# Moving a pair of two-column vector instructions from the stage that prepares a projection into the projection itself

## The chip, the cores and the metric

The kernel runs on one core of a Trainium2 chip. The metric is the device time of one execution in microseconds (us); the median of several executions is compared.

## What is computed

The input x has 1024 rows of 512 numbers. It is normalized row by row (layer norm), and two branches work on the result xn:

```python
xn = _layernorm(x, axis=-1)
s = _L0_attn_ref(xn, ...)        # attention
g = _silu(_L0_ffn_ref(xn, ...))  # feed-forward with 4-bit weights
x = x + s * g
```

The attention has 32 query heads and 8 heads of keys and values, each 128 wide, with four query heads to one key head:

```python
q = (x @ Wq.T)...; k = (x @ Wk.T)...; v = (x @ Wv.T)...
q = _rmsnorm(q, q_norm_w)
k = _rmsnorm(k, k_norm_w)
scores = jnp.einsum('bkgqd,bksd->bkgqs', qg, k) / math.sqrt(HD)
bias = jnp.where(rel > 0, NEG_INF, slopes[:, :, None, None] * rel)
attn = jax.nn.softmax(scores + bias[None], axis=-1)
out = jnp.einsum('bkgqs,bksd->bkgqd', attn, v)
return out.reshape(b, s, H * HD) @ Wo.T
```

Queries and keys are normalized by head, the values are not.

## The kernel before

Four stages follow one another: the layer norm with the gate and up projections of the feed-forward branch; its down projection; the query, key and value projections (about 220 to 505 us of the span); and the attention with the output projection and the gating. This case is about the third, and about the seams before and after it.

**Projections.** A list `projections` holds twelve of them, numbered k = 0 to 11: for each of four pairs of key heads one of keys and values (`kv`; k = 0, 3, 6, 9) and two of queries (`q`). A projection works through eight tiles of 128 rows, t = 0 to 7. `tile(t)` multiplies the tile of xn by the weights into one accumulator `ps`: twelve matmuls, since both operands are split into a high and a low half and three of the four products are taken. The accumulators have two tags ("o" for odd tiles, "m" for even ones) with two buffers each. ACT (ScalarE) then copies the queries or keys into `f` (L515) and sums their squares (L517). Of a `kv` projection, ACT also casts the values to 16 bits (`v16`, L521), and DVE (VectorE) takes the rest that the cast left out (L522). `v16` has three buffers; one step later both halves are stored to memory by two DMAs (L527). `f` has three buffers of four tiles.

**Factors of the values.** So that the values fit 16 bits, the columns of the value weights are scaled before the projection by a factor `al` for each column, found from their squares, and the attention's result is scaled back by the reciprocal. This goes in steps, and `prepare(k + 1, t)` gives the next projection's steps to the tiles of the current one: squares at t = 0, sums (`norms`) at t = 1, `scale` at t = 3, which also stores `al` to memory by a DMA (`ald`, L483), `factors` at t = 5, which loads it back by a DMA with heads as columns (`ri`, L490), and `undo` at t = 7. `undo` takes the reciprocal of `ri`, 128 x 2 numbers (L495), and multiplies it by a constant into two columns of `rv` (L496). `rv` is read by the attention alone (`heads_hi`, L807, and `heads_lo`, L813). The weights of the next projection are split into halves meanwhile (`split`, L502 on ACT and L503 on DVE). For projection 0 the same steps are given to the last iterations of the down projection (`undo` in its last one).

**Deferred steps.** What follows a tile's sums is put off by a table of due times: `finish_step()` ends each tile and runs what is due. Every four tiles `queue_half` enters the inverse root (L535, L84, L85 on DVE, Newton steps on POOL, that is GpSimd), the normalization on POOL (L556), and the split of the normalized rows into 16-bit halves `q` or `k` on DVE (`halves`, L568 and L569; `a16`, five buffers). One step later SP issues a transposing DMA (L574, into `tr`, five buffers) and two steps after that the store (L579 for queries, L582 for keys). So the halves of a projection's tiles fall four to eight tiles after them, that is into the next projection.

**Order.** Every engine runs its instructions in the order in which the program gives them; the order is written out by hand. All DMAs leave from one queue, SP's. At the start of k = 9 SP also issues the loads of the first keys, values and queries of the attention (L709, L713, L717), 512 KB each. From k = 10 on, the first steps of the attention run between the tiles.

Of the kernel before, what the change touches and what calls it, by code (L numbers as in the profile page):

```python
# [31 lines left out]
HT = NT // 2  # L32
# [35 lines left out]
def attention_gated_by_ffn_kernel(ctx, tc, x, gu_w, gu_z, gu_s, dn_w, dn_z, dn_s, wq, wkv, wo, qnw, knw, out):  # L68
# [374 lines left out]
    def finish_step():  # L443

        for f in finishing.pop(clock[0], ()):
            f()
        clock[0] += 1
# [141 lines left out]
    def prepare(k, t):  # L589

        if k < len(projections):
            p = projections[k]
            if t == 0:
                p.squares()
            elif t == 1:
                p.norms()
            elif t == 3:
                p.scale()
            elif t == 5:
                p.factors()  # L600
            elif t == 7:
                p.undo()
            if p.kind == "q" and 2 <= t < 6:
                p.split(t - 2)
            elif p.kind == "kv" and 4 <= t < 6:
                p.split(2 * t - 8)
                p.split(2 * t - 7)
# [7 lines left out]
    for it in range(3, NI):  # L615
        if it < 3 + 2 * KT:
            projections[(it - 3) // KT].load((it - 3) % KT)
        last = it == NI - 1
        gu_unit(
            it,  # L620
            None,
            it + 1 if not last else None,
            meanwhile={NI - 2: lambda: dn_dequant(0, ve), NI - 1: down_begin}.get(it, lambda: None),
            total=not last,
        )
        if it in (NI - 5, NI - 4):
            prepare(0, it - NI + 5)
        if it == NI - 3:
            dn_load(0)
            dn_load(1)  # L630
        if last:
            dn_load(2)
            dn_split_h(0, 1)
# [3 lines left out]
    for it in range(NI):  # L637
        for tb in range(2):
# [17 lines left out]
            if tb:  # L656
                if it in (1, 2):
                    gu_total((NI - 1, None), it - 1)
                elif it == 3:
                    gu_finish(0)  # L660
                elif it == 4:
                    gu_finish(1)
                elif it == 5:
                    norm_weights()
                elif it == NI - 5:
                    prepare(0, 3)
                elif it >= NI - 4:
                    prepare(0, 8 - NI + it)
# [15 lines left out]
    def queue_half(p, half):  # L684

        last = p is projections[-1]

        def due(steps, i, f):
            t = half * HT + i
            c = TILES - early + BS * (NB * (1 + t // 2) + FINISH_BLOCK) + 4 * (t % 2) if last else clock[0] + i  # L690
            finishing.setdefault(c + steps, []).append(f)

        due(0, 0, lambda: p.inverse(half))
        for i in range(3):
            due((i + 1) // 2, 0, lambda i=i: p.newton(half, i == 2))
        for i in range(HT):
            t = half * HT + i
            due(4, i, lambda t=t: p.halves(t))
            due(2, i, lambda t=t: p.normalize(t))
# [7 lines left out]
    def load_keys(g):  # L707
        kT[g] = ap1.tile([P, NT, 2, P], F16, tag="kT", name=f"kT{g}")
        sp.dma_start(kT[g].rearrange("p t a k -> p t (a k)"), kd[g].rearrange("t p c -> p t c"))  # L709

    def load_values(g):
        vT[g] = ap1.tile([P, NT, 2, HD], F16, tag="vT", name=f"vT{g}")
        sp.dma_start(vT[g].rearrange("p t a d -> p t (a d)"), vd[g])  # L713

    def load_queries(g, qb):
        qT[g, qb] = ap1.tile([P, NQT, 2, NH, P], F16, tag="qT", name=f"qT{g}_{qb}")
        sp.dma_start(  # L717
            qT[g, qb].rearrange("p t a g q -> p t (a g q)"), qd[g][qb * NQT : (qb + 1) * NQT].rearrange("t p c -> p t c")
        )
# [12 lines left out]
    def relative(g):  # L732

        trel[g] = ap1.tile([P, S], F32, tag="trel", name=f"trel{g}")
        ge.tensor_scalar(trel[g], nrel, rc, float(SLOPES[g * NH + NH - 1]), ALU.mult, ALU.mult)
# [190 lines left out]
    for k, p in enumerate(projections):  # L926
        if k == len(projections) - 3:
            load_keys(0)
            load_values(0)
            load_queries(*blocks[0])  # L930
            relative(0)
        for t in range(NT):
            prepare(k + 1, t)
            if k + 2 < len(projections) and t < KT:
                projections[k + 2].load(t)
            p.tile(t)
            finish_step()
            if t % HT == HT - 1:
                queue_half(p, t // HT)
            if k >= len(projections) - 2 and t % 2 == 0:  # L940
                step(early)
                early += 1
# [46 lines left out]
```

## Time and profile before

| what | us |
|---|---|
| median of 3 runs | 1102.81 |
| lowest and highest of them | 1100.63, 1103.02 |
| the profiled execution | 1098.13 |
| its span in the profile | 1096.4 |
| PE (TensorE, matmuls) busy | 1043.1 |
| DVE busy | 878.5 |
| ACT busy | 761.5 |
| POOL busy | 393.3 |
| the four RECIPROCALs (L495) begin between | 212.4 and 424.5 |

The span runs from the first to the last instruction of the program; what the execution takes beyond it lies around it. In the lines of a timeline the first two numbers are the start, counted from the span's start, and the duration of one row; then come the engine ("SPq" is SP's queue, which only issues), the line of the program, the operation, what it writes and reads, shapes and the number of instructions in the row. In brackets stands the idle time of the engine before it and what ended that. In the table of waits, a line says who waited for whom, and the total, the number and the longest of these waits. The chain of waits follows the work that ended last back from its end, at each step to what released it.

### The profile page before, as it was taken

How to read it: one execution, taken by the hardware profiler on the slowest of the kernel's cores; microseconds unless marked ns; L12 is line 12 of the kernel's file. 1: busy time of each engine (PE TensorE's matmuls, PEld its weight loads, DVE VectorE, ACT ScalarE, POOL GpSimd, SP SyncE). 2: the span in 40 equal slices, each digit the busy share in tenths (PEclk: the TensorE clock that was granted, in tenths of full speed). 3: DMA queues.
4: the chain of work that ended last, by engine and by line, in shares of the span. 5: the costliest groups of instructions: out<-in, count | busy, mean ns of one | idle time of the engine just before them, and what ended most of it. 6: DMA issues, size and time to landing. Idle time of an engine off the chain costs nothing.

```text
span 1096.4 us, 18629 instructions
## 1 busy us (share of the span) xinstructions
PE 1043.1 (95%) x5900; PEld 763.1 (70%) x5900; DVE 878.5 (80%) x1703; ACT 761.5 (69%) x2031; POOL 393.3 (36%) x545
## 2 busy tenths in 40 slices
PE   7999999999999999898899899999999999999997
PEld 6677678878888887675566667666666676676664
DVE  7888897537687786787789798898898987969984
ACT  5767543446666474677779688796796887868962
POOL 2566553126778787560202304004021030032222
PEclk9999999999999999899999999999999999999999
DMA  6122345146998979979989999899999998999993
GB/s 196 57 87 91 93 128 166 53 132 144 218 229 183 230 179 250 245 163 227 215 170 203 187 223 212 195 206 192 195 210 188 200 221 175 195 220 208 239 193 114
DMA packets 461632, 198.11 MB, mean 181 GB/s; under 512 B 395810, under 2 KB 421726, under 8 KB 461534
## 3 DMA queue, kind: packets, MB, share of 16 engines
q1 hardware_dynamic: 461534, 196.93, 81.6%
q8 instruction: 46, 0.75, 0.3%
q14 instruction: 52, 0.43, 0.1%
HBM read 71.03 MB, written 29.36 MB: 92 GB/s over the span
## 4 chain that ended last, share of the span: by engine, by line
PE 61%; DMA 13%; DVE 10%; ACT 8%; issue 5%; POOL 3%; SPq 0%; DVEq 0%; ACTq 0%; POOLq 0%
DMA pT<-p 12%; PE gu_ps L249 6%; PE ps_q L105 4%; PE ps_q L106 4%; PE ps_q L107 4%; PE s L105 4%; PE s L106 3%; PE s L107 3%; PE av L105 3%; PE op L105 3%; PE op L106 3%; PE op L107 3%; PE av L106 3%; PE av L107 3%; ACT p L770 3%
## 5 line engine op out<-in xcount | busy, mean ns | idle before, releaser
L779 DVE SCALAR_TENSOR_TENSOR p<-pf,row,p 128x1024 f16<-128x1024 f32 (+7 forms) x256 | 219.9, 859 | 69.3 <-ACT p L770 67.0
L770 ACT ACTIVATE p<-pf,row 128x1024 f16<-128x1024 f32 (+7 forms) x256 | 197.0, 770 | 66.6 <-DMA pT<-p 63.2
L760 ACT ACTIVATE pf<-pf,row 128x1024 f32<-128x1024 f32 (+7 forms) x256 | 197.2, 770 | 42.1 <-DVE row L759 40.2
L730 POOL TENSOR_TENSOR wol<-wor,woh 128x512 fp32r<-128x512 f32 x32 | 58.1, 1816 | 427.4 <-ACT woh L729 379.0
L759 DVE CUSTOM_DVE_ANT_0 pf<-s,trel,cs 128x1024 f32<-128x1024 f32 (+7 forms) x256 | 207.3, 810 | 3.0 <-PE s L107 2.3
L105 PE MATMUL av<-pT,vT 128*128 128x256 f16 (+1 forms) x640 | 170.8, 267 | 20.5 <-DMA pT<-p 19.9
L106 PE MATMUL av<-pT,vT 128*128 128x256 f16 (+1 forms) x640 | 168.2, 263 | 0.0
L107 PE MATMUL av<-pT,vT 128*128 128x256 f16 (+1 forms) x640 | 168.1, 263 | 0.0
L105 PEld LDWEIGHTS <-vT 128*128 128x128 f16 x640 | 62.4, 97 | 101.7 <-issue 80.6
L105 PE MATMUL s<-kT,qT 128*128 128x512 f16 (+3 forms) x384 | 125.3, 326 | 6.9 <-DVE row L759 6.6
L106 PE MATMUL s<-kT,qT 128*128 128x512 f16 (+3 forms) x384 | 125.2, 326 | 0.0
L107 PE MATMUL s<-kT,qT 128*128 128x512 f16 (+3 forms) x384 | 123.6, 326 | 0.0
L105 PE MATMUL op<-woh,oh 128*128 128x512 f32 x248 | 121.8, 491 | 0.0
L105 PE MATMUL ps_q<-wh_q,xth 128*128 128x512 f32 x256 | 101.4, 396 | 0.0
L107 PE MATMUL ps_q<-wh_q,xtl 128*128 128x512 f32 x256 | 99.8, 390 | 0.0
L106 PE MATMUL ps_q<-wl_q,xth 128*128 128x512 f32 x256 | 99.6, 389 | 0.0
L106 PE MATMUL op<-wol,oh 128*128 128x512 f32 x248 | 97.9, 395 | 0.6 <-POOL wol L730 0.6
L107 PE MATMUL op<-woh,ol 128*128 128x512 f32 x248 | 98.4, 397 | 0.0
L807 ACT ACTIVATE oh<-av,rv 128x256 fp32r<-128x256 f32 x128 | 58.9, 460 | 23.1 <-PE av L107 22.3
L556 POOL TENSOR_TENSOR f_q<-f_q,inv_q 128x512 f32<-128x512 f32 x64 | 72.8, 1155 | 1.4
L813 DVE SCALAR_TENSOR_TENSOR ol<-av,rv,oh 128x256 fp32r<-128x256 f32 x128 | 61.2, 478 | 14.2 <-ACT oh L807 14.1
L106 PEld LDWEIGHTS <-vT 128*128 128x128 f16 x640 | 63.2, 99 | 11.7 <-issue 2.3
(164 smaller groups left out, 2391.1 us busy)
## 6 DMA issues: line engine op xcount, KB each, us to landing
qd<-tr_q SPq DMA_DIRECT2D x64, 256.0 KB, 3.4
qT<-qd SPq DMA_DIRECT2D x32, 512.0 KB, 4.2
wq<-in_wq SPq DMA_DIRECT2D x32, 256.0 KB, 3.9
wor<-in_wo SPq DMA_DIRECT2D x32, 256.0 KB, 3.1
gui<-in_gu_w SPq DMA_DIRECT2D x13, 512.0 KB, 3.5
wkv<-in_wkv SPq DMA_DIRECT2D x16, 256.0 KB, 3.9
vd<-v SPq DMA_DIRECT2D x64, 64.0 KB, 2.3
kd<-tr_kv SPq DMA_DIRECT2D x64, 64.0 KB, 2.5
```

Of the source, the lines that this page charges most:

```text
L105: te.matmul(ps, lhsT=lh, rhs=rh, start=first, stop=False)
L106: te.matmul(ps, lhsT=lh, rhs=rl, start=False, stop=False)
L107: te.matmul(ps, lhsT=ll, rhs=rh, start=False, stop=last)
L249: te.matmul(banks[j][:, k, :], lhsT=w[:, j, ws], rhs=x[:, j, k * 512 : k * 512 + 512], start=x is xth, stop=x is xtl)
L556: ge.tensor_tensor(f, f, ib, ALU.mult)
L730: ge.tensor_tensor(wol[g, i], raw, woh[g, i].bitcast(F32), ALU.subtract)
L759: ve.tensor_tensor_reduce(p, ps, trel[g][:, S - w :], cs[:, hh : hh + 1], 3e38, ALU.add, ALU.min, least[:, c])
L760: se.activation(p, p, AF.Exp, bias=least[:, c], scale=-1.0, accum_out=total[:, c])
L770: se.activation(p16[u, qt][:, :, 0, :], pf[u, qt], AF.Copy, scale=scale[:, qt : qt + 1])
L779: ve.scalar_tensor_tensor(lo, p, scale, hi, ALU.mult, ALU.subtract)
L807: se.activation(oh, av_ps[u], AF.Copy, scale=rv[:, g : g + 1])
L813: ve.scalar_tensor_tensor(ol, av_ps.pop(u), rv[:, g : g + 1], oh.bitcast(F32), ALU.mult, ALU.subtract)
```

## The change

`undo` is no longer one of the steps that `prepare` gives to the projection before (t = 7). It is called in the main loop, ahead of `tile(4)` of the projection that it belongs to (HT is 4): five tiles later. The function itself is the same, and for query projections it does nothing. The DMAs that store and load the factors (L483 and L490) stay where they are. For projection 0 the pair of instructions moves from the last iteration of the down projection to tile 4 of projection 0.

```diff
@@ -598,8 +598,6 @@
                 p.scale()
             elif t == 5:
                 p.factors()
-            elif t == 7:
-                p.undo()
             if p.kind == "q" and 2 <= t < 6:
                 p.split(t - 2)
             elif p.kind == "kv" and 4 <= t < 6:
@@ -933,6 +931,8 @@
             prepare(k + 1, t)
             if k + 2 < len(projections) and t < KT:
                 projections[k + 2].load(t)
+            if t == HT:
+                p.undo()
             p.tile(t)
             finish_step()
             if t % HT == HT - 1:
```

## The prediction

> **What bounds the kernel now.** I read the page first, to see which engine carries the span.
>
> ```profile
> span 1096.4 us, 18629 instructions
> PE 1043.1 (95%) x5900; PEld 763.1 (70%) x5900; DVE 878.5 (80%) x1703; ACT 761.5 (69%) x2031; POOL 393.3 (36%) x545
> ```
>
> PE is busy for 95% of the span, so only what makes PE idle, or slows its clock, costs time. The change touches two small DVE instructions (L495 and L496) of each of the four key and value projections. So I asked what these wait for and what PE waits for near them. The table of waits for 405 to 450 us, the turn from projection 8 (the last but three) to projection 9 (the last of keys and values), holds both:
>
> ```profile
> ACT v L521 <- DMA vd<-v: 11.5, 3, 8.3
> ACT f_kv L515 <- DVE q L569: 8.2, 2, 7.1
> DVE ri L495 <- DMA ri<-ald: 4.2, 1, 4.2
> PE ps_kv L105 <- DVE v L522: 4.1, 1, 4.1
> ```
>
> The columns are total, times, longest. Read upwards: PE stood 4.1 us for a DVE instruction, and 4.2 us of DVE's time went into the wait that the change takes away. In all of the projections (232 to 505 us) the table has no other PE wait but one of 0.5 us. The question of this case is whether these two lines are one chain. The timelines of that turn, engine by engine, say. DVE:
>
> ```profile
> 418.89 1.41 DVE L569 TENSOR_TENSOR q<-f_q,q 128x512 f16<-128x512 f32 x1
> 424.46 0.17 DVE L495 RECIPROCAL ri<-ri 128x2 f32<-128x2 f32 x1 [4.17 <-DMA ri<-ald]
> 424.66 0.74 DVE L496 TENSOR_SCALAR rv<-ri 128x2 f32<-128x2 f32 x1
> 425.31 0.41 DVE L568 CAST q<-f_q 128x512 f16<-128x512 f32 x1
> 425.76 1.50 DVE L569 TENSOR_TENSOR q<-f_q,q 128x512 f16<-128x512 f32 x1
> ```
>
> ACT, which needs the f buffer that the last of these frees:
>
> ```profile
> 427.37 0.37 ACT L515 COPY f_kv<-ps_kv 128x256 f32<-128x256 f32 x1 [7.12 <-DVE q L569]
> ...
> 431.49 0.48 ACT L515 COPY f_kv<-ps_kv 128x256 f32<-128x256 f32 x1
> ...
> 440.81 0.37 ACT L521 CAST v<-ps_kv 128x256 f16<-128x256 f32 x1 [8.31 <-DMA vd<-v]
> ```
>
> SP, the queue of all DMAs:
>
> ```profile
> 421.67 0.51 SPq L490 DMA_DIRECT2D ri<-ald  x1
> 422.23 0.55 SPq L579 DMA_DIRECT2D qd<-tr_q  x1
> ...
> 431.60 2.46 SPq L574 DMA_TRANSPOSE tr_q<-q  x1
> 434.10 0.61 SPq L464 DMA_DIRECT2D wq<-in_wq  x1
> 434.75 0.48 SPq L579 DMA_DIRECT2D qd<-tr_q  x1
> 435.33 0.90 SPq L527 DMA_DIRECT2D vd<-v  x2
> ```
>
> PE:
>
> ```profile
> 437.24 0.39 PE L107 MATMUL ps_kv<-wh_kv,xtl 128*128 128x512 f32 x1
> 441.69 0.80 PE L105 MATMUL ps_kv<-wh_kv,xth 128*128 128x512 f32 x1 [4.06 <-DVE v L522]
> ```
>
> The reader is to see two delays one after the other on ACT. DVE's wait holds ACT until 427.37. But ACT then runs through tiles 0, 1 and 2 of projection 9 and is stopped again at tile 3 (its copy of f at 431.49, its cast of v only at 440.81), and this second stop comes from SP. v16 has three buffers, so the cast of tile 3 needs tile 0's stores (L527) landed; they leave SP at 435.33 and 435.76 and land 4.94 us after the second issue, at 440.7 (chain of waits). PE's accumulators come from two tags of two buffers, so PE runs four tiles ahead of ACT and DVE: it stops at tile 7, for the accumulator of tile 3.
>
> **The change part by part.** Removed from `prepare`: four RECIPROCALs (median 162 ns, with the next start 0.2 us on) and four TENSOR_SCALARs (median 170 ns), about 0.35 us a pair and 0.85 us where it started at 424.46 and the next instruction at 425.31. They are added again at tile 4: DVE's busy sum changes by 0.
>
> The wait that goes: L495 waits 4.8 us in 2 of its 4 places, 4.17 at 424.46 and 0.65 at 353.69. What is late next on DVE is L568 of projection 7's last tile. Its input from POOL ended before 419.8 (row 418.53 + 1.22). Its output q has five buffers, so it needs the transpose of five tiles before, issued at 417.56; transposes land 2.4 to 5.1 us after issue (median 3.3), and SP's store of that tile, which needs it too, left at 422.23. So L568 moves from 425.31 to about 422.2, a gain of 3.1 us on DVE and not 4.17 + 0.85. ACT's 427.37 becomes about 424.3.
>
> What that is worth to PE: the cast of tile 3 would be ready to run from about 429 rather than 432, and still waits for 440.7. For that to move, the stores must leave SP sooner. Nothing that the change touches issues a DMA: ald (L483) and ri (L490) keep their places. SP runs its rows end to start from 421.67 to 435.33, with gaps of 0.2 us or less, and is about four tiles late: the ri DMA belongs to a tile whose matmuls began at 410.4 and left at 421.67. Its transpose at 431.60 had its data at 427.27, and the store at 435.33 at 428.99: 4.3 and 6.3 us early, before the change. So a DVE that is 3.1 us earlier releases nothing on SP. I take 0 for the gain. The upper bound for this term is the transpose of 2.46 us against 1.29 for the median of its kind: were the 1.17 us a hidden wait on DVE, PE would gain 1.2 us.
>
> The Trainium skill's page Perfetto Trace Analysis (DMA Instruction, HWDGE) states that such a row starts when its semaphores are satisfied, and holds the lock and descriptors alone; by it the 1.17 us is no wait and the gain is 0, by the rows alone 0 to 1.2 us.
>
> What is added at tile 4: in projection 9 the pair stands in DVE's queue behind wl_q (442.61 + 0.68) and ahead of v of tile 4 (L522 at 444.00, idle 0.70 before it). Of 0.35 to 0.85 us, at most 0.15 is not in that idle time. Behind it wait ACT for f, SP for v, and PE for the accumulator: v of tile 4 ends at 444.42 and the matmuls that reuse its buffer start at 446.96, a margin of 2.5 us. Cost 0; uncovered it would be 0.85. ri landed at 424.44, some 18 us before, so no wait comes with it. In projections 0 and 3, v of tile 4 starts after 1.50 and 0.70 us of idle time on DVE, which hide the pair; in projection 6 (v at 370.36) it has none, so DVE is up to 0.35 us later there, and PE, which shows no idle time in that projection, has four accumulators between. The readers of rv (L807, L813) start at 511.8, 67 us after the last write.
>
> Sum: 0, between -1.2 and +0.85. The profiled execution took 1098.13 us (span 1096.4 and 1.73 around it), 4.7 below the median of the three runs; I apply the sum to that median, 1102.81. About 0.2%, 2.2 us, is what a measurement of this kernel can tell from no change.
>
> **The rivals.** *Faster: the two delays are one.* For it speaks that the chain of waits does run from the vd store back through DVE to the ri DMA, and that the runs are slower than the profiled one, so that ACT may have less slack there. Then PE's stall shrinks from 4.06 by the 3.1 us to about 1, and the slow clock behind it goes: the 12 matmuls of the tile after the stall took 441.69 to 446.96, 5.27 us, where a tile takes 2.72 (ACT's copies at 405.03 and 407.75); that is 2.55 us. Together 5.65: 1097.1 us; with the whole stall 6.6: 1096.2. Against it: SP's rows, above. It decides if the stores at 435.33 leave earlier.
>
> How short a stall keeps the clock: idle times of 1.50 at 39.5 left a granted clock of 1.00 (38 to 44 us), one of 2.07 at 23.4 was followed by 0.50 (24 to 27). So a stall of 1 us pays no clock.
>
> The skill's page TensorE: Matmul & The Clock Gate (Part 1) puts the drop after an idle window of about 3.4 us; by it any stall under 3.4 us would save the 2.55, by the rows only one under about 2 us. In this rival both give the same; were only 1.2 us gained (a stall of 2.9), the rule would give 3.75 us, just outside the bound, and the rows 1.2.
>
> *Slower: the wait moves along.* If L495 at tile 4 finds a wait as long as the one it had (4.17 us), it stands ahead of v of tile 4. The margin is 2.5 us, so PE stalls 1.6 us there, and with the slow clock going on for a further tile (2.55) 4.2: 1104.4 to 1107.0 us. It decides from 2.5 us on. For it: DVE's queue is in order, and the queue of DMAs is full there (DMA share 1.13 in 441.7 to 447). Against: the 18 us since ri landed.
>
> *The wait changes its name only.* DVE stands at 420.3 anyway, for the transpose's landing. That is in my forecast for 1.9 of the 4.17 us; were it all, the time is again 1102.8.
>
> **How the numbers follow.** No change: 0.52. Its own range is 1100.6 to 1105.0. Faster 0.32, as the one large idle time of PE in the projections is three steps from the wait removed. Slower 0.16. The time is 1102.8. Downwards the range goes to 1097.0, which leaves out the faster cases that win the whole stall, about a third (0.1); upwards to 1106.0, which leaves out the worst of the slower ones, 0.08.
>
> **What would show it.** Right: L495 without idle time in projection 9 at tile 4; L568 near 422.2 by the same clock, with "DMA tr_q<-q" ahead of it; ACT's f_kv near 424.3; ACT's wait for vd longer, about 11 us; SP's rows from ri to vd unmoved; PE's stall still some 4 us, with 0.5 of the clock behind it. Wrong: vd leaving SP earlier against tile 0's matmuls, PE's stall under 2 us, or a new PE wait at the start of projection 10.

## The result and the profile after

The time does not change: 1102.97 us against 1102.78 (medians of 14 runs each), a ratio of 1.000 with an interval of 0.9988 to 1.0013. Runs of one kernel lie some 5 us apart, so that the profiled executions (1100.69 us with a span of 1098.9 after, 1098.13 with 1096.4 before) differ by no more than two runs of one kernel do.

The page first. PE is as busy as it was, DVE 2.4 us less:

```profile
span 1098.9 us, 18629 instructions
PE 1043.2 (95%) x5900; PEld 764.0 (70%) x5900; DVE 876.1 (80%) x1703; ACT 762.6 (69%) x2031; POOL 390.8 (36%) x545
```

The table of waits for 410 to 450 us, the turn to projection 9 (total, times, longest):

```profile
ACT v L521 <- DMA vd<-v: 13.8, 2, 10.7
DVE v L522 <- ACT v L521: 10.6, 4, 6.7
...
PE ps_kv L105 <- DVE v L522: 4.4, 1, 4.4
...
DVE q L568 <- DMA tr_q<-q: 0.3, 1, 0.3
```

DVE's wait of 4.17 us for ri is gone, and of the transpose that was to be late next 0.3 us are seen. ACT's wait for the value stores is longer by 2.4 us, and PE's stall is what it was. DVE's timeline of the same turn:

```profile
421.86 0.43 DVE L568 CAST q<-f_q 128x512 f16<-128x512 f32 x1 [0.25 <-DMA tr_q<-q]
422.32 0.69 DVE L569 TENSOR_TENSOR q<-f_q,q 128x512 f16<-128x512 f32 x1
...
443.77 0.16 DVE L495 RECIPROCAL ri<-ri 128x2 f32<-128x2 f32 x1
443.97 0.17 DVE L496 TENSOR_SCALAR rv<-ri 128x2 f32<-128x2 f32 x1
444.56 0.42 DVE L522 TENSOR_TENSOR v<-ps_kv,v 128x256 f16<-128x256 f32 x1 [0.43 <-ACT v L521]
```

The last tile's halves are 3.4 us earlier, and the pair stands at tile 4 without a wait of its own and with 0.43 us of idle time still left behind it. ACT's timeline:

```profile
423.12 0.38 ACT L515 COPY f_kv<-ps_kv 128x256 f32<-128x256 f32 x1 [2.61 <-POOL inv_q L550]
...
441.37 0.37 ACT L521 CAST v<-ps_kv 128x256 f16<-128x256 f32 x1 [10.71 <-DMA vd<-v]
```

ACT starts projection 9 4.25 us earlier (427.37 before) and is stopped at the same tile 3, to the same moment within 0.6 us. The first row names POOL's L550, which ended last by the profile (422.44 + 0.66); the buffer that the copy writes was read last by DVE's L569, which ended at 423.01. SP's queue says why the second stop stays where it was:

```profile
421.76 0.57 SPq L490 DMA_DIRECT2D ri<-ald  x1
...
431.87 2.11 SPq L574 DMA_TRANSPOSE tr_q<-q  x1
...
435.36 0.95 SPq L527 DMA_DIRECT2D vd<-v  x2
```

These rows started at 421.67, 431.60 and 435.33 before. The transpose's data was ready at 427.27 then and is ready at 423.01 now (422.32 + 0.69): 4.3 us earlier, and it leaves no earlier. And PE, with the row of the windows behind its stall (PE, PEld, DVE, ACT and POOL busy; granted clock; DMA share; GB/s):

```profile
442.25 0.80 PE L105 MATMUL ps_kv<-wh_kv,xth 128*128 128x512 f32 x1 [4.37 <-DVE v L522]
```

```profile
442.20:447.50 5.30, 5.25 (x12) 4.18 (x13) 4.34 (x12) 2.54 (x13) 0.79 (x2) 0.50 1.44 230
```

### The profile page after: what moved, and what is told of

The parts are those of the page before. It is cut to its first block, busy times and chain, and to the rows that moved or that the text cites. A ratio compares the mean times of both kernels' runs of the same rounds, so it can differ in the third digit from the quotient of the medians.

```text
span 1098.9 us, 18629 instructions
## 1 busy us (share of the span) xinstructions
PE 1043.2 (95%) x5900; PEld 764.0 (70%) x5900; DVE 876.1 (80%) x1703; ACT 762.6 (69%) x2031; POOL 390.8 (36%) x545
## 4 chain that ended last, share of the span: by engine, by line
PE 53%; DMA 15%; DVE 13%; ACT 8%; issue 6%; POOL 5%; SPq 1%; DVEq 0%; ACTq 0%; POOLq 0%
DMA pT<-p 12%; PE gu_ps L249 6%; PE s L105 3%; PE s L106 3%; PE s L107 3%; PE av L105 3%; PE op L105 3%; PE op L106 3%; PE op L107 3%; ACT p L768 3%; PE ps_q L107 3%; PE av L107 3%; PE av L106 3%; PE ps_q L105 3%; PE ps_q L106 3%
## 5 line engine op out<-in xcount | busy, mean ns | idle before, releaser
L105 PE MATMUL av<-pT,vT 128*128 128x256 f16 (+1 forms) x640 | 171.0, 267 | 23.4 <-DMA pT<-p 23.4
L105 PEld LDWEIGHTS <-vT 128*128 128x128 f16 x640 | 62.4, 97 | 103.8 <-issue 78.1
L105 PE MATMUL s<-kT,qT 128*128 128x512 f16 (+3 forms) x384 | 125.3, 326 | 6.6 <-DVE row L757 6.2
L105 PE MATMUL op<-woh,oh 128*128 128x512 f32 x248 | 122.0, 492 | 0.0
L105 PE MATMUL ps_q<-wh_q,xth 128*128 128x512 f32 x256 | 101.6, 397 | 0.0
```

Source lines behind the costliest of these rows:

```text
L105: te.matmul(ps, lhsT=lh, rhs=rh, start=first, stop=False)
```

## The experiments

The theory: the wait for ri lies in slack, and SP's late queue sets PE's stall. Its main rival: both delays are one chain, so that the wait does cost time, if only in part. Below, the length of projection 9 is from its first matmul to the first of projection 10: 28.5 us before and 28.9 after the change; eight tiles of 2.72 us at full speed are 21.8. Such lengths and all other times of rows come from one profiled execution of each kernel. Each kernel is compared with the kernel before on the same chip. The runs stand here in the order of the questions.

**Is the wait in slack once the stall is gone?** If the three v16 buffers are what ties ACT to SP, five of them remove the stall, and a chain that hid behind it would then show. Room for them was made by two changes that leave the arithmetic as it is: the two broadcast weights share the tag, and the squares, which are never read, go into one buffer instead of four.

```diff
-    qwb = wp.tile([P, HD], F32, name="qwb")
+    qwb = wp.tile([P, HD], F32, tag="v16", name="qwb", bufs=5)     # kwb too
-    self.jk = wp.tile([P, NH, HD], BF16, ...)
+    self.jk = wp.tile([P, HD], BF16, ...)
-    v16 = wp.tile([P, 2, 2, HD], F16, tag="v16", ..., bufs=3)
+    v16 = wp.tile([P, 2, 2, HD], F16, tag="v16", ..., bufs=5)
```

It was put on the kernel after (first) and on the kernel before (second).

> The changed kernel with five buffers for v16 instead of three (room is made by one shared buffer for the unused squares and by giving the two norm weights v16's buffers). Stores theory (PE's stall in projection 9 is set by the value stores of tile 0, three buffers before): ACT's cast of tile 3 no longer waits, the next to wait is tile 5's, whose accumulator PE needs only at tile 1 of projection 10, about 443 us; PE's idle time of 4.4 us at 442 us goes, and the half clock behind it (2.5 us). If nothing takes its place the time falls by up to 6.9, to about 1096 us. Given-back theory (the start of the attention is bound by DMAs anyway): the stall goes, but idle time of PE between 490 and 530 us grows by as much, and the time stays within 2 us of the kernel before.

> The kernel before, with the old place of the reciprocal, and v16 with five buffers as in the run beside it. Stores theory: DVE still waits about 4 us for ri and ACT's copy of f still comes near 427, but tile 3 is cast at about 432.5 and its accumulator is free at 433, before PE wants it at 437.6; no stall, and the same time as the changed kernel with five buffers, within 2.2 us. One-chain theory (DVE's wait reaches PE once the stores are out of the way): PE idles 2 us or more in projection 9 here and not in the other, and this one is 2 to 6 us slower than it.

Measured: 1102.92 us (ratio 1.0002, 0.9985 to 1.0019) and 1101.55 (0.9994, 0.9976 to 1.0013). In both, projection 9 takes 21.8 us and has no PE wait. So the three buffers did tie PE to SP. The second still has the wait for ri, 2.54 us at 423.54, and does not lose by it. But neither kernel gains the 6.8 us that projection 9 is shorter: PE now waits 4.73 and 4.08 us at 461.7, for DVE's first row of the attention ("PE s L105 <- DVE row"). The stall was a symptom, and the cause still had to be found.

**What does the wait cost at other places?** On the kernel before, `undo` one step earlier (t = 6), and two (t = 5, right behind `factors`, ahead of the split of the next weights).

```diff
-            elif t == 7:
+            elif t == 6:
                 p.undo()
```

```diff
             elif t == 5:
                 p.factors()
-            elif t == 7:
                 p.undo()
```

> The kernel before with the reciprocal one tile earlier (tile 6 of the projection before). DVE's wait for ri in front of projection 9 grows from 4.2 to about 6 us, with the halves of two tiles behind it instead of one; ACT's copy of f moves from 427.4 to about 429.3. Stores theory: ACT still has some 6 us in hand at tile 3, PE's stall stays near 4.1 us, and the time stays within 2.2 us of before. One-chain theory: PE's stall grows by the 1.9 us, to 6, and the time by 2.

> The kernel before with the reciprocal at tile 5, right behind the load of ri and ahead of the split of the last two weight rows of the next projection. DVE waits about 8.3 us in front of projection 9 (416.1 to 424.5), and now PE stands behind it: the low halves of the weights come at about 426, wanted at 419.9. Stores theory: PE stalls some 6.3 us at the start of projection 9, but reaches tile 7 so much later that the stores have landed, so the stall of 4.1 us there goes; with about 1 us in projection 6 the time grows by only 2 to 4 us. If the stalls simply add up, it grows by 8 to 10 us.

At t = 6: 1100.91 us (0.9993, 0.9976 to 1.001). The wait is longer, 8.6 us in two places and 5.04 of them at projection 9, and the time does not change: PE's stall comes in two parts, 1.12 us at 429.42 and 3.49 at 441.38, together 4.6, and projection 9 takes 28.6 us.

At t = 5: 1110.13 us (1.0062, 1.004 to 1.0084), slower. Three waits, 14.0 us. DVE's timeline of this kernel, and PE's:

```profile
427.87 0.17 DVE L495 RECIPROCAL ri<-ri 128x2 f32<-128x2 f32 x1 [7.55 <-DMA ri<-ald]
...
428.73 2.13 DVE L503 TENSOR_TENSOR wl_kv<-wkv,wh_kv 128x512 fp32r<-128x512 f32 x2
```

```profile
429.46 0.49 PE L106 MATMUL ps_kv<-wl_kv,xth 128*128 128x512 f32 x1 [4.15 <-DVE wl_kv L503]
```

PE needs the lower half of the weights for the first tile, and the split now stands behind the wait. Here the one-chain rival is true: 7.55 us on DVE become 4.15 on PE. Yet projection 9 is no longer for it (28.5 us), because its later stall is gone: PE pays once, at the one place or the other. The loss arises in projection 6, where nothing was to be paid before: 26.8 us instead of 21.8, with waits of 2.46 and 0.49 us behind a wait of 6.16 on DVE. Projection 10 takes 1.8 us more (28.7 and 26.9). The two make up the 6.8 us that the ratio stands for; the medians lie 9.1 us apart.

**Is it the load of the turn?** The SP queue has three loads for the attention (512 KB each) in just this turn. They were moved two turns ahead, to the start of projection 5; `relative(0)` stays where it was. First on the kernel after, then on the kernel before.

```diff
+        if k == 5:
+            load_keys(0); load_values(0); load_queries(*blocks[0])
         if k == len(projections) - 3:
-            load_keys(0); load_values(0); load_queries(*blocks[0])
             relative(0)
```

> The changed kernel with the first loads of keys, values and queries of the attention (three DMAs of 512 KB) issued at the start of projection 5 instead of projection 9. Queue theory (SP's queue and its DMAs set the turn into projection 9, and with more buffers the wait only moved behind it): the three rows of 1.7 us and their 1.5 MB are out of the way, the stores of tile 0 leave SP about 432 instead of 435.4 and land at about 435, ACT's cast of tile 3 is in time and PE's idle time of 4.4 us at 442 falls below 1; projection 9 takes 22 us instead of 28.8. Unlike with five buffers SP itself is ahead by 2 to 5 us, so half or more of it stays: the time falls by 3 to 6 us. Given-back theory: projection 9 is shorter, but PE's idle time before 530 us grows by as much and the time stays within 2 us.

> The kernel before, with the reciprocal in its old place, and the same three loads at the start of projection 5. Queue theory: DVE waits for ri as before (about 4 us, the loads were behind ri on the queue), ACT starts projection 9 near 427.4, and PE still has no stall: within 2.2 us of the changed kernel with early loads. One-chain theory: now that the stores come in time, the wait is next; PE idles 2 us or more in projection 9 and this one is slower by 2 to 6.

Measured: 1101.65 us (1.0005, 0.9991 to 1.0019) and 1102.11 (1.001, 0.9998 to 1.0022); the 3 to 6 us that the queue theory expected did not come. Projection 9 becomes shorter, 24.7 and 22.9 us, and projections 7 and 8 longer: 45.1 and 49.4 us together where the kernel before takes 44.1. Counted from the first matmul of projection 9, the first of the vd stores leaves SP after 14.9 us in the first kernel (435.91), where it left after 16.7 in the kernel after: 1.8 us less, about what the three rows had taken (428.95 to 430.86); the rest of the delay stays. The load that is taken out of one turn is paid in the ones before. The wait for ri in the second was 8.9 us in two places, without a difference in time that could be told from the first. That it takes 4 us more in projections 7 and 8 is in good part one stop of PE there: 2.45 us at 403.88, for squares of the next weights (L469) which ACT began late because it waited 2.38 us for the load of these weights, with half the clock for 3.41 us behind it. In the first kernel the same stop is 0.88 us. Why the load came later is open.

**Is it SP's queue?** Then fewer rows in it should bring time where room in buffers brought none. The 64 stores of the values were given to ACT's queue: the same bytes, and 64 rows less on SP.

```diff
-                sp.dma_start(vd[2 * self.i + i][:, t, :], ...)
+                se.dma_start(vd[2 * self.i + i][:, t, :], ...)
```

It was put on the kernel after, on the same with the early loads, on the kernel before, and on the kernel after with five v16 buffers and the one squares buffer.

> The changed kernel with the stores of the values (64 DMAs) issued from ACT's queue instead of SP's. Queue theory: they leave one tile after their cast, near 427 in projection 9, and no longer wait for some 11 us of rows before them on SP; the stall at 442 goes, projection 9 takes 22 to 24 us, and SP has 0.9 us less to issue for each tile of keys and values, so it falls behind less and the wait does not come back in full: the time falls by 2 to 6 us. If ACT's issuing (0.9 us a tile at SP's price) makes ACT late, PE idles in small pieces in projections 0, 3, 6 and 9 and the time rises by up to 4.

> The changed kernel with both: early loads and stores from ACT's queue. Queue theory: the best of the set, with projection 9 at 22 us and no idle time of PE over 1 us between 418 and 500; 4 to 8 us below the kernel before. Given-back theory: the time again within 2 us, with PE's idle time gone to the first 40 us of the attention.

> The kernel before, with the reciprocal in its old place, and the stores of the values from ACT's queue. Queue theory: with fewer rows on SP the load of ri leaves earlier (at 416.5 in the changed kernel with ACT's stores, against 421.8), so DVE's wait in front of projection 9 shrinks by itself to under 1 us, and the place of the reciprocal makes no difference: 3 to 5 us below the kernel before, within 2.2 us of the changed kernel with the same stores. One-chain theory: with the stores out of the way the old place costs 2 us or more against the new one.

> The changed kernel with the stores of the values from ACT's queue and five buffers for v16. If the stores' landing still sets the turn into projection 9, its idle time of 1.5 us at 442 goes and the time falls by up to 2 us against three buffers. If the transposes on SP do (DVE's halves wait for their buffers, as with five buffers alone), the time is the same as with three, within 2.2 us.

| kernel | us | the kernel before beside it | ratio | projection 9, us |
|---|---|---|---|---|
| after, ACT stores | 1095.82 | 1100.84 | 0.9965 (0.9949 to 0.9981) | 23.4 |
| the same, early loads | 1098.54 | 1100.84 | 0.9984 (0.9964 to 1.0004) | 21.8 |
| before, ACT stores | 1095.81 | 1101.96 | 0.9948 (0.993 to 0.9967) | 21.8 |
| after, ACT stores, v16 five, one squares buffer | 1101.41 | 1101.96 | 0.9991 (0.9971 to 1.001) | 21.8 |

This step gains on the kernel before, with the reciprocal at either place: 3.9 us with the new one (0.0035 of 1100.84) and 5.7 with the old (0.0052 of 1101.96); the intervals of the two overlap. ACT's wait for vd between 221 and 500 us, 19.7 us in eight places before and 23.9 in nine after, is 1.3 us in three places in the kernel after with ACT stores. On the kernel before, the wait for ri is gone by itself, since its load now leaves SP 3.5 us earlier (421.67 before). SP's and DVE's timelines of that kernel:

```profile
418.17 0.89 SPq L490 DMA_DIRECT2D ri<-ald  x1
```

```profile
423.79 0.15 DVE L495 RECIPROCAL ri<-ri 128x2 f32<-128x2 f32 x1
```

The stores are not free on ACT. In the kernel after with ACT stores, ACT stands 4.13 us while it issues the two stores of one tile ("ACTq" is ACT's queue); what held the second was not followed up:

```profile
425.60 4.09 ACTq L527 DMA_DIRECT2D vd<-v  x2
429.73 0.62 ACT L502 CAST wh_q<-wq 128x512 fp32r<-128x512 f32 x1 [4.13 <-DVE inv_q L84]
```

And PE waits 1.0 us in projection 8 for ACT's squares of the next weights (1.6 in the kernel before with ACT stores); with SP's stores it waited 0.3 there after the change and not at all before.

The early loads missed: they had been expected to be the best of the set. In the profiled executions projections 6 to 8 took 70.5 us with them, and 66.9 and 68.6 without (after, before); but the intervals with and without them overlap, so that a loss by them is not shown. With the five buffers the stall is gone, and so is the gain.

**Was that the buffers or the squares?** With one buffer for the squares, ACT's four of a tile began 0.40 us apart (402.20 and 402.60 in the kernel after with five v16 buffers); each takes 0.28 us. The last two kernels give the squares two buffers in turn, and five to v16, on the kernel after without and with the ACT stores.

```diff
-    se.activation(self.jk, ...)
+    se.activation(self.jk[:, i % 2], ...)      # jk is [P, 2, HD]
```

> The changed kernel with five buffers for v16 as before, but the room is made by two buffers for the unused squares instead of one. One buffer had a price of its own: with it ACT's squares start every 0.40 us instead of 0.25, about 0.45 us more for each tile of queries. If that price hid a gain, the squares are at 0.25 us again and the time falls by 3 to 7 us against the kernel before. Queue theory: the stall at 442 goes again and comes back behind it, where DVE waits for the landing of transposes; within 2.2 us of the kernel before.

> The changed kernel with the values' stores from ACT's queue, and five buffers for v16 with the squares in two buffers. If the one buffer for the squares cost the four us that separate five buffers (1101.4) from three (1095.8) with ACT's stores, the time is back at 1095 to 1097. If five buffers cost them themselves, it stays near 1101.

Measured: 1100.34 us (0.9994, 0.9977 to 1.0011) and 1097.0 (0.9967, 0.9946 to 0.9988). The squares begin 0.26 us apart (405.14 and 405.40). With them the five buffers do no harm to the ACT stores, though the intervals with one and with two squares buffers still touch (up from 0.9971, down from 0.9988), so that this cause is likely and not settled. For it speaks the table of PE's waits: with ACT stores and one squares buffer PE waits 5.3 us in three places for ACT's squares of the next weights (L469), with two 0.7 in one. The five buffers add nothing that can be told from the ACT stores alone.

The first of the two shows where the gain of a removed stall goes. It is the cleanest such kernel: from 221 to 500 us the table of PE's waits has one line,

```profile
PE s L105 <- DVE row L757: 3.8, 1, 3.8
```

and the timelines of DVE and of SP ahead of it are these:

```profile
454.95 0.29 DVE L568 CAST k<-f_kv 128x256 f16<-128x256 f32 x1 [1.55 <-DMA tr_q<-q]
...
458.76 1.15 DVE L757 CUSTOM_DVE_ANT_0 pf<-s,trel,cs 128x896 f32<-128x896 f32 x1
```

```profile
448.86 1.24 SPq L574 DMA_TRANSPOSE tr_q<-q  x1
450.19 0.52 SPq L579 DMA_DIRECT2D qd<-tr_q  x1
450.81 0.89 SPq L527 DMA_DIRECT2D vd<-v  x2
451.75 1.24 SPq L574 DMA_TRANSPOSE tr_q<-q  x1
```

SP's rows follow each other within 0.1 us, and a tile's share (a transpose, a store of its result, two value stores) comes back after 2.89 us; the next tiles do the same, at 454.64 and 457.53. PE needs 2.72 us for a tile. So SP cannot make up a delay while PE runs at full speed, and loses 0.17 us more on each such tile. How large the delay is, the end of a tile's halves (L569) and the start of its transpose (L574) tell, taken in order. For tiles 4 to 7 of projection 8 the transpose leaves this long after its data:

| profiled kernel | us |
|---|---|
| before (behind PE's stall) | 3.8 to 5.1 |
| v16 five, two squares buffers | 8.6 to 9.8 |
| after, ACT stores | 1.3 to 1.5 |
| before, ACT stores | 0.9 to 1.9 |

With the five buffers the stall no longer gives SP time, the q buffers come free late (DVE waits 3.1 us in three places for a transpose), and DVE reaches the first row of the attention late. Three starts of PE's matmuls, by kernel, give the sum:

| profiled kernel | first of projection 10 | last of the projections (L105 start) | last score matmul (L105 start) | span |
|---|---|---|---|---|
| before | 447.0 | 500.1 | 1067.7 | 1096.4 |
| after | 447.5 | 501.1 | 1070.3 | 1098.9 |
| v16 five, two squares buffers | 439.8 | 499.4 | 1070.3 | 1098.5 |
| after, ACT stores | 442.2 | 497.2 | 1065.4 | 1092.4 |
| before, ACT stores | 443.1 | 498.3 | 1066.2 | 1093.7 |
| ACT stores, v16 five, two squares buffers | 440.0 | 498.1 | 1064.1 | 1091.4 |

The five buffers put projection 10 7.2 us earlier than before, and 0.7 us of it is left at the end of the projections. The ACT stores keep 1.8 to 2.9 us, or 1.1 to 2.2 when each kernel is counted from its own first projection matmul (220.7 before, 219.8 to 220.8 with them). What lies beyond 500 us differs by up to 5 us between single executions (566.0 to 570.9 from the one column to the next), so that the table doesn't say where the rest of their gain is.

## Why the prediction was right

*No gain, since the wait lies in slack* (forecast, 1102.8 us): 1102.97. Shown twice over: by the rows of the kernel after (DVE earlier by 3.4 us, SP's rows at their old times), and by the pairs with and without the wait, which agree with five buffers and with the early loads (with the ACT stores no wait is left to compare). With `undo` at t = 6 an even longer wait cost nothing.

*What is late next on DVE*: forecast the transpose's landing, L568 at 422.2; measured 421.86 behind 0.25 us of that wait. ACT's copy of f came at 423.12 and not 424.3, 1.2 us earlier: I had left L569 its 1.50 us, and it took 0.69, which is the median of its kind in both kernels. Nothing hung on it.

*ACT's wait for vd about 11 us, SP unmoved, PE's stall some 4 us at half the clock*: 10.71; 0.03 to 0.27 us; 4.37 at 0.50.

*The transpose of 2.46 us*, which was to cap a hidden wait on DVE at 1.2 us: 2.11, with its data 4.3 us earlier. What the Trainium skill's page Perfetto Trace Analysis (DMA Instruction, HWDGE) states, that such a row starts only when its semaphores are satisfied, agrees with this row: the long row was no wait for its data from DVE. (The page counts the sequencer's own semaphore increments into the row too, beside the lock and the descriptors that the prediction named.) The forecast of 0 for that term holds.

*The pair at tile 4, at most 0.15 us of it uncovered*: it was covered wholly, with 0.43 us of idle time to spare in projection 9. L495 shows no idle time ahead of it at any of its four places, so the slower rival, the wait that moves along, had nothing to start from. DVE's busy sum, forecast as unchanged, fell by 2.4 us; where was not followed up.

*The term that was mis-sized* stands in the faster rival, which put 5.65 to 6.6 us on the removal of the stall and the half clock behind it. Five buffers took 6.8 us out of projection 9, and the time stayed. The price of a stall was read from its own stage; the queue that caused it still had the same work, and asked for the time 20 us later, at 460. The five-buffer kernels say that even with the whole stall gone the time would have been about the same, so that most of the chance of 0.32 belonged to no change.

*How short a stall keeps the clock* was read from two idle times, 1.50 us (1.00) and 2.07 (0.50), as a limit of about 2 us. That reading does not hold: in the same trace 2.04 us of idle time at 11.06 was followed by 1.00 (11 to 15 us). The forecast did not use it; the price of 2.55 us for the stall at hand was read from its own row.

What is not settled: in the turn itself (421 to 435 us) the runs do not separate the rows' issue time from the landings that some of them wait for; the back-to-back pitch of 2.89 us is shown for the tiles from 448 to 460. Nor do they separate two things that the ACT stores change at once, 64 rows less on SP and stores that leave earlier (in projection 9 1.6 to 3.4 us after their data, 4.1 to 9.7 before).

## What to carry to other kernels

A wait that is taken away is worth what the next late thing leaves of it: find that first, on the engine itself and on the engine that stops last, and look whether its releaser had its data long before it ran. If it did, the cause is a queue and not an engine; add up the rows that the queue issues for a tile, compare the sum with the time PE needs for it, and take rows off the queue before buffers are added, since buffers only move the stall to where the queue is next needed. An instruction that waits for a DMA costs what stands behind it: here a wait of 6.16 us ahead of the split of weights made projection 6 5.0 us longer, and the wait of 4.17 us two steps later, in projection 9, cost nothing.

## What had not been expected of the hardware

The half clock came after shorter idle times of PE than the 3.4 us of the skill's page TensorE: Matmul & The Clock Gate (Part 1): 0.50 behind 2.07 and 2.88 us (the kernel before at 23.43; with ACT stores, five v16 and two squares buffers at 459.79). But the length of one idle time does not decide it here. It was 1.00 behind 1.12 and 1.49 us, and behind 3.52 us too (ACT stores, five v16 buffers, one squares buffer, at 405.18). The clearest pair are the two kernels with five v16 buffers and one squares buffer, where PE waits equally long at the same place. First the kernel after, then the kernel before, the PE row and the row of the windows behind it:

```profile
510.05 0.38 PE L105 MATMUL s<-kT,qT 128*128 128x512 f16 x1 [2.25 <-DVE row L757]
```

```profile
511.30:514.50 3.20, 2.41 (x21) 1.90 (x22) 1.90 (x5) 2.41 (x5) 0.00 (x0) 1.00 1.16 216
```

```profile
509.99 0.38 PE L105 MATMUL s<-kT,qT 128*128 128x512 f16 x1 [2.25 <-DVE row L759]
```

```profile
511.30:514.50 3.20, 3.20 (x14) 2.01 (x15) 2.71 (x6) 2.54 (x6) 0.00 (x0) 0.50 1.02 188
```

What all fourteen traces share is how long a drop lasts: 3.41 us, or two or three times that (6.83 and 10.24), apart from drops that reach the end of the program. The drop at the stall of the kernel before lasts 6.83 us from 440.11, so that it begins 1.6 us before PE goes on.

Activations of 128x128 that write one and the same buffer one after the other began 0.40 us apart, and 0.26 with two buffers in turn, at the same 0.28 us each.
